# The state-space mixing with channels on partitions, and its roots on VectorE

## The chip, the cores and the metric

The kernel runs on one core of a Trainium2 chip. The metric is the time of one execution on the device in microseconds (us), as the median of several runs. Everything is fp32. The engines are named as the profile names them: PE is TensorE (PEld its weight loads), DVE is VectorE, ACT is ScalarE, POOL is GpSimd and SP is SyncE, which here only starts transfers.

## The reference, cut to what matters

Two layers work on 8 sequences of 256 tokens with 256 features, 2048 tokens in all. After each of the four parts the input is added and a layer norm is taken.

```python
x = layernorm(x + attention(x))              # 16 heads of 128
x = layernorm(x + experts0(x))               # 32 experts, 6 per token, and a shared one
x = layernorm(x + state_space(x))            # the part that the change touches
x = layernorm(x + experts1(x))               # 16 experts, 4 per token, and a shared one

def state_space(x):                          # E = 512 channels, 8 heads of 64, N = 64
    gate, hBC, dt = split(x @ in_proj_w.T)
    h, B, C = split(silu(causal_conv(hBC, 4 taps)))
    dt = softplus(dt + dt_bias);  a = -exp(A_log) * dt
    # per head, over the tokens s <= l of one sequence:
    y[l] = sum_s (C[l].B[s]) * exp(sum of a over s+1..l) * dt[s] * h[s]  +  D * h[l]
    yf = y * silu(gate)
    yn = norm_w * yf * rsqrt(mean(yf * yf over the 512 channels) + 1e-6)
    return yn @ out_proj_w.T
```

The sum over s is taken in blocks of 128 tokens. A sequence has two blocks: within a block a product of matrices, and for the second block the contribution of a state S that the first block leaves (called "the state's part" here).

## The kernel before

The kernel is one program for all of it. Tokens are taken in 4 groups (g) of 512, each of 4 tiles (t) of 128 tokens, so a group holds two sequences. The residual x of a group lies in SBUF with tokens on partitions (`xg[g]`). The order of the work in the program text is written out by hand with generators: `weave` takes several of them, gives each a start and an end on an axis of "slots", and calls them in turn. The tile framework's scheduler then threads the instructions on each engine, so that an engine's order is not quite that of the text; within the finished program every engine's queue runs in order.

**The state-space layer.** `front(g)` prepares a group: transposes x (`turned_group`, L1256), projects and convolves it (`convolved`, L1194 to L1203, channels on partitions), takes the time steps (`time_steps`, L1214 to L1245, a long chain of tiny VectorE steps that ends in `dta`), the decays (`decays`: `edge` L1275, and per tile and four heads a matmul `sg` L1305 with an exponential that gives the block's decay matrix e), the product of B and C (`gm`, L1337) and the gate (`gtp`, L1361, then the silu of L1179). The gate has tokens on partitions, one tile of 128x512 per t. `back(lo, hi)` runs the slots. In slot s, four things are done for four different tiles, s, s-1, s-2 and s-3:

- tile s: transposes h (L1393), multiplies by dt (`hd`, L1399) and, in even tiles, by the decay to the block's end (`hx`, L1405); multiplies e by gm (L1411, twice); in even tiles it forms the state S (L1419, copied by ACT L1424).
- tile s-1: `y`, tokens on partitions: for every pair of heads a matmul of h with `dres`, a diagonal matrix of D (L1438), and on top of it one matmul per head (L1443), with the 128x128 matrix of the head as weights and 64 columns of `hd` streaming. In odd tiles the state's part `yo` (L1451) is scaled by `edge` (L1455) and added (L1460). Then the product with the gate (L1462 or L1464), the square with its sum over the row by ACT (L1469), and its root.
- tile s-2: four transposes of yf (L1484) and ACT's copy `yfT` (L1486).
- tile s-3: the output projection (L1494), the residual with the root as factor (L1498), and the layer norm (`normed`).

A matmul of fp32 is two instructions on PE, a transpose is one. PSUM is given out by tag: "a" 3 banks, "b" 2 (hdp, Sp, yfp, out), "c" 2 (y), "d" 1 (yo).

**Roots.** `normed` (L726) computes 1/sqrt(var + eps). In groups 0 to 2 POOL does it in three steps (L741, L742 with the operation pow, L744), and the root of the squares' mean too (L1475). In the last group `root_by_steps` (L713) does both on VectorE: a first guess by integer arithmetic and three Newton steps, 11 tiny instructions per root. After either, ACT applies it to x (L745).

**Around it.** `all_combined(g)` finishes the first mixture of experts for a group and also calls `normed`. `routed_group(g)` runs `route` for the second mixture, once tile 3 of group g is through: transposes of the new x (L299), logits (L307), the choice, and 16 scatters of rows by POOL (L380), each preceded by POOL's copy of the row (L375). After the slots come the shared expert (`sh1.shared`, and for groups 1 and 2 L552 and L572), the route of group 3, and the routed tiles: SP loads 128 rows per tile, PE works, POOL scatters the result (L680). The weights of the second mixture's experts are loaded into the big buffer `big` by SP as places in it become free: `order` (L1154) names these places, and `load_up_to` after slot s loads as many experts as fit into those that are free by then. A routed tile picks its expert at run time and so needs all of them loaded.

## Time and profile before

| | |
|---|---|
| median of 6 runs | 1513.46 us (1512.56 to 1518.49) |
| the profiled execution | 1512.64 us |
| its span, first to last instruction | 1510.9 us |
| granted TensorE clock, mean | 0.968 |
| PE busy | 1419.3 us (94%) |
| VectorE busy | 816.2 us (54%) |
| ACT busy | 547.4 us (36%) |
| POOL busy | 486.1 us (32%) |

How to read the profile. Times are microseconds from the first instruction of the span. A line of the timeline has start, length, engine, source line, operation, output and inputs, and shape (partitions x elements); in brackets stands how long the engine was idle before it, and what ended the idle time. "x8" means eight instructions merged into one line. A busy PE is modelled, since matmuls overlap; the starts of weight loads are the better clock for it. A group line has busy us, the mean of one in ns, and the idle time before the group's instructions. The granted clock is the share of full speed that TensorE was allowed.

### The profile page before, as it was taken

The numbers are of one execution on the slowest core, as the hardware profiler recorded it, in microseconds if no ns is written. First come the engines' busy times: TensorE is split into PE (matmuls) and PEld (weight loads), VectorE is DVE, ScalarE is ACT, GpSimd is POOL, SyncE is SP. The second block draws the span as 40 slices with busy tenths as digits, with TensorE's granted clock in tenths as the row PEclk, the third lists the DMA queues.
The fourth block names the chain that finished last, engine by engine and source line by source line (L and its number), as shares of the span: only waits on it lengthen the run. The fifth ranks groups of instructions, "written<-read, shape, count | busy, mean of one in ns | idle before, by whom it ended". The sixth has DMA issues, their size and how long they took to land.

```text
span 1510.9 us, 21640 instructions
## 1 busy us (share of the span) xinstructions
PE 1419.3 (94%) x6482; PEld 1010.8 (67%) x6482; DVE 816.2 (54%) x2957; ACT 547.4 (36%) x1447; POOL 486.1 (32%) x736
## 2 busy tenths in 40 slices
PE   8999999999999999997999994899998699999997
PEld 4666666676666666676778883555666577777766
DVE  3444465456544465456455554676674664544436
ACT  3333342333333342334244442455554222333323
POOL 1000003500152001522755664022144555643345
PEclk9999999999999999998999997899998889999999
DMA  9999999930010001343555555310000622333327
GB/s 362 411 413 414 412 407 392 345 77 1 11 53 22 0 1 60 109 152 104 148 183 157 160 167 193 103 65 1 1 25 32 250 102 86 111 108 95 96 75 278
DMA packets 79974, 233.51 MB, mean 155 GB/s; under 512 B 11323, under 2 KB 44378, under 8 KB 78448
## 3 DMA queue, kind: packets, MB, share of 16 engines
q1 hardware_dynamic: 60784, 187.79, 34.8%
q0 software_dynamic: 16768, 42.19, 7.9%
q10 hardware_dynamic: 2304, 2.10, 0.4%
q8 instruction: 56, 0.92, 0.3%
q14 instruction: 62, 0.51, 0.1%
HBM read 80.29 MB, written 155.40 MB: 156 GB/s over the span
## 4 chain that ended last, share of the span: by engine, by line
PE 62%; issue 14%; POOL 13%; DMA 5%; DVE 4%; ACT 1%; POOLq 1%; SPq 0%; ACTq 0%; DVEq 0%
PE qkp L943 15%; PE vp L927 7%; PE op L1009 6%; POOL m1ys L680 5%; PE zp L996 4%; PE sc L963 4%; POOL m1xs L380 3%; PE pt L990 3%; DMA m0ys<-m0ys,m0xl 2%; PE sc L959 2%; PE sg L1305 2%; PE zp L1000 2%; PE cv L1194 2%; POOL m0ys L680 1%; PE gtp L1361 1%
## 5 line engine op out<-in xcount | busy, mean ns | idle before, releaser
L943 PE MATMUL qkp<-xT,big 128*128 128x512 f32 x512 | 241.2, 593 | 0.0
L978 ACT ACTIVATE pr<-neg,least 128x128 f32<-128x128 f32 (+1 forms) x256 | 114.4, 448 | 283.7 <-DVE least L973 283.7
L951 DVE COPY qk<-qkp 128x512 f32<-128x512 f32 x64 | 44.2, 690 | 178.2 <-PE qkp L943 178.1
L943 PEld LDWEIGHTS qkp<-xT,big 128*128 128x128 f32 x512 | 90.7, 191 | 69.4 <-issue 67.9
L680 POOL DMA_INDIRECT m0ys<-m0ys,m0xl x114 | 112.5, 986 | 65.2 <-ACT m0ys L679 26.7
L380 POOL DMA_INDIRECT m0xs<-m0xe,m0rows x96 | 94.8, 987 | 110.1 <-DVE total L982 37.9
L927 PE MATMUL vp<-big,xT 128*128 128x512 f32 x256 | 118.6, 602 | 4.6 <-DVE x L1014 4.6
L1009 PE MATMUL op<-big,z 128*128 128x256 f32 x512 | 120.5, 382 | 0.0
L973 DVE CUSTOM_DVE_ANT_0 neg<-sc,cmask 128x128 f32<-128x128 f32 (+1 forms) x256 | 81.4, 355 | 59.9 <-PE sc L963 59.2
L680 POOL DMA_INDIRECT m1ys<-m1ys,m1xl x74 | 72.8, 984 | 100.0 <-ACT m1ys L679 92.8
L1009 PEld LDWEIGHTS op<-big,z 128*128 128x128 f32 x512 | 92.6, 190 | 14.9 <-ACT z L1031 4.8
L259 POOL TENSOR_TENSOR rstd<-rstd,numbers 128x1 f32<-128x1 f32 x16 | 8.7, 551 | 280.3 <-DVE rstd L258 280.3
L927 PEld LDWEIGHTS vp<-big,xT 128*128 128x128 f32 x256 | 47.3, 193 | 49.8 <-issue 42.5
L996 PE MATMUL zp<-pT,big 128*128 128x256 f32 x256 | 76.8, 381 | 0.1
L963 PE MATMUL sc<-qk,qk 128*128 128x256 f32 x256 | 76.5, 380 | 0.0
L984 DVE TENSOR_SCALAR pr<-pr,total 128x128 f32<-128x128 f32 (+1 forms) x256 | 72.4, 331 | 3.4
L380 POOL DMA_INDIRECT m1xs<-m1xe,m1rows x64 | 63.3, 989 | 19.1 <-POOL m1xe L375 11.9
L990 PEld LDWEIGHTS pt<-ident,pr 128*128 128x128 f32 x384 | 47.4, 142 | 32.4 <-issue 29.8
L994 DVE COPY pT<-pt 128x384 f32<-128x384 f32 x128 | 66.9, 549 | 2.9 <-PE pt L990 2.1
L996 PEld LDWEIGHTS zp<-pT,big 128*128 128x128 f32 x256 | 47.7, 190 | 30.4 <-issue 12.0
L745 ACT ACTIVATE x<-x,off,rstd 128x256 f32<-128x256 f32 x48 | 28.6, 599 | 95.1 <-POOL off L744 82.4
L741 POOL TENSOR_SCALAR rstd<-mv 128x1 f32<-128x1 f32 x44 | 14.4, 329 | 140.6 <-DVE mv L732 99.2
(2809 smaller groups left out, 3093.0 us busy)
## 6 DMA issues: line engine op xcount, KB each, us to landing
m0xs<-blank SPq DMA_DIRECT2D x9, 7740.0 KB, 59.6
m1xs<-blank SPq DMA_DIRECT2D x4, 7740.0 KB, 56.5
m0xl<-m0xs SPq DMA_DIRECT2D x114, 129.0 KB, 2.3
m0gy<-m0ys SPq DMA_DIRECT2D x16, 768.0 KB, 4.3
m1xl<-m1xs SPq DMA_DIRECT2D x74, 129.0 KB, 2.2
big<-m1ys SPq DMA_DIRECT2D x16, 512.0 KB, 6.7
big<-in_w_moe SPq DMA_DIRECT2D x1, 5472.0 KB, 17.4
big<-in_w_heads SPq DMA_DIRECT2D x12, 384.0 KB, 8.0
```

The costliest lines, as they stand in the source:

```text
L380: ins = nc.gpsimd.indirect_dma_start(out=d["xs"], out_offset=bass.IndirectOffsetOnAxis(ap=rows[:, k, t : t + 1], axis=0), in_=xe[:, k, :], ...
L680: ins = nc.gpsimd.indirect_dma_start(out=d["ys"], out_offset=bass.IndirectOffsetOnAxis(ap=row[:, DM : DM + 1].bitcast(I32), axis=0), in_=y ...
L927: nc.tensor.matmul(ps, lhsT=xT[:, k, t * P : (t + 1) * P], rhs=w_vq[q][:, k, :], start=(k == 0), stop=(k == KC - 1),)
L943: nc.tensor.matmul(ps, lhsT=w_qk[h][:, at : at + P], rhs=xT[:, k, :], start=(k == 0), stop=(k == KC - 1),)
L963: nc.tensor.matmul(sc[:, P:], lhsT=qT[:, c0 + P : c0 + SEQ], rhs=kT[:, c0 : c0 + SEQ], start=True, stop=True,)
L973: nc.vector.tensor_tensor_reduce(out=neg[:, cols], in0=sc[:, cols], in1=cmask[:, cols], scale=-SCALE, scalar=3.0e38, op0=ALU.add, op1=ALU.min,
L978: nc.scalar.activation(pr[:, cols], neg[:, cols], AF.Exp, bias=least[:, i : i + 1], scale=-1.0, accum_out=total[:, i : i + 1],)
L984: nc.vector.tensor_scalar_mul(pr[:, cols], pr[:, cols], total[:, i : i + 1])
L990: nc.tensor.transpose(pt[:, i * P : (i + 1) * P], pr[:, i * P : (i + 1) * P], ident)
L994: pace[0] = nc.vector.tensor_copy(pT, pt)
L996: nc.tensor.matmul(zps[:, b * SEQ : (b + 1) * SEQ], lhsT=vs[2 * b][:, cols], rhs=pT[:, : 2 * P], start=True, stop=False,)
L1009: nc.tensor.matmul(ps[:, :DM], lhsT=zs[i][:, t * P : (t + 1) * P], rhs=w_o[q * QH + i], start=(i == 0), stop=(i == QH - 1),)
```

## The change

`y` is now formed with channels on partitions. For each pair of heads j there is a 128x128 region of y: the rows 0 to 63 belong to the even head, 64 to 127 to the odd one. The head's matmul swaps its operands: 64 columns of `hd` are the weights, and the head's 128x128 matrix streams. The diagonal matrix `dres` and its matmuls are gone; VectorE adds D times h to y with one `scalar_tensor_tensor` per pair of heads, four per tile, D being a factor per partition. The state's part is formed a slot earlier, scaled by `edge` into a buffer `o`, and in odd tiles added to y by a matmul with the identity, which transposes it as well. The gate is projected with channels on partitions, for a whole group at once. So yf has channels on partitions, and the output projection takes it as it is: the transposes `yfp` and ACT's copies `yfT` are gone. The sum of squares over the channels is now a sum over partitions: ACT writes the squares, and in slot s PE multiplies those of tile s-2 with a column of ones, four matmuls of one column. All roots of the slots are taken by VectorE: in one slot the root of the squares of tile s-2 and the root of the variance of tile s-3 stand side by side in a 128x2 tile and go through `root_by_steps` together, 14 instructions (11 where only one of them is there). `normed` stays on POOL for the combined tokens. The places in `big` are given out anew: the two buffers `r` move out of it, `o` comes in, the gate takes 8 places instead of 7, and experts are loaded after slots 12 to 17 instead of 12 to 16.

```diff
@@ -712,18 +712,38 @@
     def root_by_steps(y, v):
 
-        work = small.tile([P, 2], F32, name="newton", tag="newton", bufs=1)
-        i, t = work[:, 0:1].bitcast(I32), work[:, 1:2]
+        n = y.shape[1]
+        work = small.tile([P, 4], F32, name="newton", tag="newton", bufs=1)
+        i, t = work[:, :n].bitcast(I32), work[:, 2 : 2 + n]
         nc.vector.tensor_single_scalar(i, v.bitcast(I32), 1, ALU.arith_shift_right)
         nc.vector.tensor_scalar(i, i, -1.0, float(0x5F3759DF), ALU.mult, ALU.add)
-        last = work[:, 0:1]
+        last = work[:, :n]
         for _ in range(3):
-            nc.vector.scalar_tensor_tensor(t, last, v, last, ALU.mult, ALU.mult)
+            if n == 1:
+                nc.vector.scalar_tensor_tensor(t, last, v, last, ALU.mult, ALU.mult)
+            else:
+                nc.vector.tensor_mul(t, last, v)
+                nc.vector.tensor_mul(t, t, last)
             nc.vector.tensor_scalar(t, t, -0.5, 1.5, ALU.mult, ALU.add)
             nc.vector.tensor_mul(y, last, t)
             last = y
 
-    def normed(g, t, by_steps=False):
+    def spread(g, t, var):
+
+        st = small.tile([P, 6], F32, name="st", tag="st")
+        nc.vector.bn_stats(st, xg[g][:, t, :])
+        mv = small.tile([P, 2], F32, name="mv", tag="mv")
+        nc.vector.bn_aggr(mv, st)
+        nc.vector.tensor_scalar_add(var, mv[:, 1:2], LN_EPS)
+        return mv
+
+    def scaled(g, t, mv, rstd):
+        x = xg[g][:, t, :]
+        off = small.tile([P, 1], F32, name="off", tag="lnoff")
+        nc.vector.scalar_tensor_tensor(off, mv[:, 0:1], -1.0, rstd, ALU.mult, ALU.mult)
+        nc.scalar.activation(x, x, AF.Identity, bias=off, scale=rstd)
+
...
@@ -1142,20 +1156,14 @@
         shsb = st.enter_context(tc.tile_pool(name="shsb", bufs=3, reuse_waits="tile"))
         HB = 4
         FRONT, BACK, COMBINE, ROUTE = 24, 36, 8, 20
-
-        dres = act.tile([P, ED // P, P], F32, name="dres", tag="dres")
-        for j in range(ED // P):
-            nc.vector.tensor_scalar_mul(
-                dres[:, j, :], ident, par[:, DRES0 + j : DRES0 + j + 1]
-            )
         ready = set()
 
 
         order, free = [], {}
         for s, names in (
-            (12, "x0 x1 x2 x3 c0 c1 r0 r1 B h0 h1 h2 h3 e8 e9 e10 e11 g2 g3 g4 m0 C0"),
-            (13, "e0 e1 g5"), (14, "e2 e3 g6"), (15, "e4 e5 g0"),
-            (16, "e6 e7 g1 h4 h5 h6 h7 m1 C1"),
+            (12, "x0 x1 x2 x3 c0 c1 B h0 h1 h2 h3 e8 e9 e10 e11 m0 C0"),
+            (13, "e0 e1 g0 g1 g2 g3"), (14, "e2 e3"), (15, "e4 e5"),
+            (16, "e6 e7 h4 h5 h6 h7 m1 C1 o"), (17, "g4 g5 g6 g7"),
         ):
             order += names.split()
             free[s] = len(order)
@@ -1290,7 +1298,7 @@
             f["e"] = {}
             for t in range(GT):
                 for q in range(HS // HB):
-                    r = slots_of("r", 2).rearrange("p (h s) -> p h s", h=HB)
+                    r = act.tile([P, HB, P], F32, name=f"r{g}_{t}_{q}", tag="r", bufs=2)
                     if q:
             yield
-            f["gate"] = []
-            for t in range(GT):
-                ps = bank("a", f"gtp{g}_{t}")
+            assert g < 2 or ("squared", (g - 2) * GT + 3) in ready
+            gate = f["gate"] = slots_of("g", 8, ED // P).rearrange("p (j s) -> p j s", s=GN)
+            for j in range(ED // P):
+                ps = bank("a", f"gtp{g}_{j}")
                 for k in range(KC):
                     nc.tensor.matmul(
-                        ps, lhsT=xT[:, k, t * P : (t + 1) * P], rhs=win[:, k, :ED],
+                        ps, lhsT=win[:, k, j * P : (j + 1) * P], rhs=xT[:, k, :],
                         start=(k == 0), stop=(k == KC - 1),
                     )
-                gt = slots_of("g", 7, last=g * GT + t)
-                curve(gt, ps, AF.Silu, exps, silus)
-                f["gate"].append(gt)
+                curve(gate[:, j, :], ps, AF.Silu, exps, silus)
                 yield
 
...
+                roots = small.tile([P, 2], F32, name=f"roots{s}", tag="roots", bufs=4)
+                has = [1, 1]
                 if s < NG * GT:
                     g, t = divmod(s, GT)
                     assert ("front", g) in ready and (s == 0 or ("slot", s - 1) in ready)
@@ -1424,71 +1435,78 @@
-                if 0 <= s - 1 < NG * GT:
-                    g, t = divmod(s - 1, GT)
-                    f = got[g]
-                    y = bank("c", f"y{g}_{t}")
-                    hd = hds.pop(t)
-                    for q in range(HS // HB):
-                        m = ms.pop((t, q))
-                        for i in range(HB):
-                            h = q * HB + i
-                            j = h // 2
-                            if h % 2 == 0:
-                                nc.tensor.matmul(
-                                    y[:, j * P : (j + 1) * P],
-                                    lhsT=f["h"][j][:, t * P : (t + 1) * P],
-                                    rhs=dres[:, j, :], start=True, stop=False,
-                                )
-                            nc.tensor.matmul(
-                                y[:, h * PD : (h + 1) * PD], lhsT=m[:, i, :], rhs=hd[:, h, :],
-                                start=False, stop=(h % 2 == 1),
-                            )
-                        yield
-                    yf = act.tile([P, ED], F32, name=f"yf{g}_{t}", tag="yf", bufs=2)
-                    if t % 2:
+                    else:
+
                         ps = bank("d", f"yo{g}_{t}")
                         nc.tensor.matmul(
                             ps, lhsT=f["C"][:, t * P : (t + 1) * P], rhs=states.pop(t - 1),
                             start=True, stop=True,
                         )
+                        yo = slots_of("o", 1).rearrange("p (h d) -> p h d", d=PD)
                         nc.vector.tensor_mul(
-                            yf.rearrange("p (h d) -> p h d", d=PD),
-                            ps.rearrange("p (h d) -> p h d", d=PD),
-                            f["edge"][:, t, :].unsqueeze(2).broadcast_to([P, HS, PD]),
+                            yo, ps.rearrange("p (h d) -> p h d", d=PD),
+                            f["edge"][:, t, :].unsqueeze(2).broadcast_to(wide),
                         )
-                        nc.vector.tensor_add(yf, yf, y)
+                        offs[t] = yo.rearrange("p h d -> p (h d)")
                         yield
-                        nc.vector.tensor_mul(yf, yf, f["gate"][t])
-                    else:
-                        nc.vector.tensor_mul(yf, y, f["gate"][t])
+                if 0 <= s - 1 < NG * GT:
+                    g, t = divmod(s - 1, GT)
+                    f = got[g]
+
+                    y = bank("c", f"y{g}_{t}").rearrange("p (j s) -> p j s", s=P)
+                    hd = hds.pop(t)
+                    tok = slice(t * P, (t + 1) * P)
+                    off = offs.pop(t, None)
+                    yf = act.tile([P, ED // P, P], F32, name=f"yf{g}_{t}", tag="yf", bufs=3)
+                    for q in range(HS // HB):
+                        m = ms.pop((t, q))
+                        for j in range(q * HB // 2, (q + 1) * HB // 2):
+                            if off is not None:
+                                nc.tensor.matmul(
+                                    y[:, j, :], lhsT=off[:, j * P : (j + 1) * P], rhs=ident,
+                                    start=True, stop=False,
+                                )
+                            for i in range(2):
+                                h = 2 * j + i
+                                nc.tensor.matmul(
+                                    y[i * PD : (i + 1) * PD, j, :], lhsT=hd[:, h, :],
+                                    rhs=m[:, h - q * HB, :], start=off is None, stop=True,
+                                )
+                        yield
+                    for j in range(ED // P):
+                        nc.vector.scalar_tensor_tensor(
+                            yf[:, j, :], f["h"][j][:, tok], par[:, DRES0 + j : DRES0 + j + 1],
+                            y[:, j, :], ALU.mult, ALU.add,
+                        )
+                        if j == 1:
+                            yield
+                    gate = f["gate"][:, :, tok]
+                    nc.vector.tensor_mul(yf, yf, gate)
                     yfs[t] = yf
+
+                    pace[0] = nc.scalar.activation(gate, yf, AF.Square)
                     ready.add(("mixed", s - 1))
-
-                    rms = small.tile([P, 1], F32, name=f"rms{g}_{t}", tag="rms")
-                    pace[0] = nc.scalar.activation(f["gate"][t], yf, AF.Square, accum_out=rms)
-                    nc.vector.tensor_scalar(rms, rms, 1.0 / ED, RMS_EPS, ALU.mult, ALU.add)
-                    if g == NG - 1:
-                        square, rms = rms, small.tile([P, 1], F32, name=f"rr{t}", tag="rms")
-                        root_by_steps(rms, square)
-                    else:
-                        nc.gpsimd.tensor_tensor(rms, rms, root[:, :1], ALU.pow)
-                    rmss[t] = rms
                     yield
                 if 0 <= s - 2 < NG * GT:
                     g, t = divmod(s - 2, GT)
-                    ps = bank("b", f"yfp{g}_{t}")
-                    yf = yfs.pop(t)
+
+                    ps = bank("b", f"squares{g}_{t}")[:, :1]
+                    square = got[g]["gate"][:, :, t * P : (t + 1) * P]
                     for j in range(ED // P):
-                        cols = slice(j * P, (j + 1) * P)
-                        nc.tensor.transpose(ps[:, cols], yf[:, cols], ident)
-                    yfT = act.tile([P, ED // P, P], F32, name=f"yfT{g}_{t}", tag="yfT", bufs=2)
-                    nc.scalar.copy(yfT.rearrange("p j n -> p (j n)"), ps)
-                    yfTs[t] = yfT
+                        nc.tensor.matmul(
+                            ps, lhsT=square[:, j, :], rhs=ones[:, :1],
+                            start=(j == 0), stop=(j == ED // P - 1),
+                        )
+                    nc.vector.tensor_scalar(
+                        squares[:, 0:1], ps, 1.0 / ED, RMS_EPS, ALU.mult, ALU.add
+                    )
+                    rmss[t] = roots[:, 0:1]
+                    has[0] = 0
+                    ready.add(("squared", s - 2))
                     yield
                 if 0 <= s - 3 < NG * GT:
                     g, t = divmod(s - 3, GT)
-                    yfT = yfTs.pop(t)
+                    yfT = yfs.pop(t)
                     ps = bank("b", f"out{g}_{t}")[:, :DM]
                     for j in range(ED // P):
                         nc.tensor.matmul(
@@ -1498,8 +1516,14 @@
                     nc.vector.scalar_tensor_tensor(
                         xg[g][:, t, :], ps, rmss.pop(t), xg[g][:, t, :], ALU.mult, ALU.add
                     )
-                    normed(g, t, by_steps=g == NG - 1)
+                    mv = spread(g, t, squares[:, 1:2])
+                    has[1] = 2
                     yield
+                if has[0] < has[1]:
+                    cols = slice(*has)
+                    root_by_steps(roots[:, cols], squares[:, cols])
+                if has[1] == 2:
+                    scaled(g, t, mv, roots[:, 1:2])
                 ready.add(("slot", s))
                 load_up_to(M1, free.get(s, 0) * SLOT)
 
```

(In `normed` the branch with `by_steps` is removed; what is left are the POOL steps L741 to L744 and L745.)

More of the change, by code (lines that the diff above doesn't have):

```diff
@@ L724, in root_by_steps, with normed @@
             last = y
-    def normed(g, t, by_steps=False):
+    def spread(g, t, var):
[10 more added lines that the diff above has]
+        nc.scalar.activation(x, x, AF.Identity, bias=off, scale=rstd)
+    def normed(g, t):
         x = xg[g][:, t, :]
@@ L734, in normed @@
         off = small.tile([P, 1], F32, name="off", tag="lnoff")
-        if by_steps:
-            var = small.tile([P, 1], F32, name="var", tag="rstd")
-            nc.vector.tensor_scalar_add(var, mv[:, 1:2], LN_EPS)
-            root_by_steps(rstd, var)
-            nc.vector.scalar_tensor_tensor(off, mv[:, 0:1], -1.0, rstd, ALU.mult, ALU.mult)
-        else:
-            nc.gpsimd.tensor_scalar_add(rstd, mv[:, 1:2], LN_EPS)
-            nc.gpsimd.tensor_tensor(rstd, rstd, root[:, :1], ALU.pow)
-            nc.vector.tensor_scalar_mul(off, mv[:, 0:1], -1.0)
-            nc.gpsimd.tensor_tensor(off, off, rstd, ALU.mult)
+        nc.gpsimd.tensor_scalar_add(rstd, mv[:, 1:2], LN_EPS)
+        nc.gpsimd.tensor_tensor(rstd, rstd, root[:, :1], ALU.pow)
+        nc.vector.tensor_scalar_mul(off, mv[:, 0:1], -1.0)
+        nc.gpsimd.tensor_tensor(off, off, rstd, ALU.mult)
         nc.scalar.activation(x, x, AF.Identity, bias=off, scale=rstd)
@@ L1380, in front @@
             ready.add(("front", g))
-        ms, hds, states, yfs, yfTs, rmss = {}, {}, {}, {}, {}, {}
+        ms, hds, states, offs, yfs, rmss = {}, {}, {}, {}, {}, {}
         def back(lo, hi):
             for s in range(lo, hi):
+                squares = small.tile([P, 2], F32, name=f"squares{s}", tag="squares")
+                roots = small.tile([P, 2], F32, name=f"roots{s}", tag="roots", bufs=4)
+                has = [1, 1]
                 if s < NG * GT:
@@ L1465, in back @@
                     yfs[t] = yf
+                    pace[0] = nc.scalar.activation(gate, yf, AF.Square)
                     ready.add(("mixed", s - 1))
-                    rms = small.tile([P, 1], F32, name=f"rms{g}_{t}", tag="rms")
-                    pace[0] = nc.scalar.activation(f["gate"][t], yf, AF.Square, accum_out=rms)
-                    nc.vector.tensor_scalar(rms, rms, 1.0 / ED, RMS_EPS, ALU.mult, ALU.add)
-                    if g == NG - 1:
-                        square, rms = rms, small.tile([P, 1], F32, name=f"rr{t}", tag="rms")
-                        root_by_steps(rms, square)
-                    else:
-                        nc.gpsimd.tensor_tensor(rms, rms, root[:, :1], ALU.pow)
```

## The prediction

> **What bounds the kernel now.** First the busy time of each engine by stretch of the span. The columns are: stretch and its length in us, then busy us of matmuls, weight loads, VectorE (DVE), ScalarE (ACT) and GpSimd (POOL), each with its number of instructions, the granted TensorE clock, the DMA share and GB/s.
>
> ```profile
> 980.00:1250.00 270.00, 241.69 (x1148) 167.07 (x1147) 178.91 (x653) 122.52 (x258) 98.39 (x190) 0.91 0.19 70
> 1165.00:1197.00 32.00, 31.55 (x193) 24.66 (x192) 25.78 (x126) 14.76 (x35) 12.01 (x23) 1.00 0.57 222
> 1151.00:1163.00 12.00, 12.00 (x42) 8.83 (x43) 4.96 (x16) 3.24 (x10) 1.53 (x4) 0.52 0.00 1
> 1210.00:1224.00 14.00, 13.92 (x47) 10.88 (x46) 6.84 (x60) 4.71 (x9) 6.57 (x12) 0.53 0.22 66
> 1300.00:1460.00 160.00, 160.00 (x775) 118.70 (x774) 72.83 (x214) 50.61 (x128) 66.27 (x68) 1.00 0.33 101
> ```
>
> The state-space slots lie at about 980 to 1250 us. TensorE is busy 241.7 of those 270 us, VectorE 178.9 (66%). From 1300 to 1460, the second mixture of experts, TensorE never stops, so a microsecond that TensorE saves in the slots reaches the end whole, as long as the experts' rows are there in time. Two stretches run at about half clock; the waits and the timeline tell why. A waits line gives us in total, times, the longest.
>
> ```profile
> ACT x L745 <- POOL off L744: 44.6, 13, 12.9
> PE m1xTp L299 <- ACT x L745: 12.7, 2, 12.1
> PE hdp L1393 <- ACT yfT L1486: 4.0, 1, 4.0
> ```
>
> ```profile
> 1203.29 0.98 POOL L380 DMA_INDIRECT m1xs<-m1xe,m1rows  x1 [0.28 <-POOL m1xe L375]
> 1204.64 0.22 POOL L741 TENSOR_SCALAR rstd<-mv 128x1 f32<-128x1 f32 x1
> 1205.03 1.07 POOL L380 DMA_INDIRECT m1xs<-m1xe,m1rows  x1 [0.17 <-DMA m1xs<-m1xe,m1rows]
> 1206.47 0.59 POOL L742 TENSOR_TENSOR rstd<-rstd,numbers 128x1 f32<-128x1 f32 x1
> 1207.37 1.06 POOL L380 DMA_INDIRECT m1xs<-m1xe,m1rows  x1 [0.17 <-issue]
> 1208.81 0.20 POOL L744 TENSOR_TENSOR off<-off,rstd 128x1 f32<-128x1 f32 x1
> ...
> 1209.69 0.69 PE L299 MATMUL m1xTp<-ident,x 128*128 128x128 f32 x2 [12.09 <-ACT x L745]
> ...
> 1149.83 0.60 ACT L745 ACTIVATE x<-x,off,rstd 128x256 f32<-128x256 f32 x1 [8.81 <-POOL off L744]
> 1150.95 0.44 PE L1393 MATMUL hdp<-ident,big 128*128 128x128 f32 x2 [4.04 <-ACT yfT L1486]
> ```
>
> The three tiny steps of a layer norm (L741, L742, L744) stand in POOL's queue among the scatters of the router. The mean and variance were ready at about 1194.3 (bn_aggr starts at 1194.13, 0.18 long), the last POOL step ran at 1208.8. Until then ACT is blocked, and TensorE idle for 12.09 us. At 1147 to 1151 it is the same: ACT stands 8.81 us at the norm, the copy yfT behind it frees no bank, and TensorE waits 4.04 us. After each gap the clock is 0.52 or 0.53 for 12 and 14 us: 0.48 x 12 = 5.8 and 0.47 x 14 = 6.6 us lost. The two stalls cost 12.1 + 6.6 + 4.0 + 5.8 = 28.5 us.
>
> **Part 1: roots leave POOL.** All norms of the slots (groups 0 to 2; group 3 already) get their roots on VectorE. The POOL roots that stay (combined tokens of groups 2 and 3) run before the first scatters at 1117, so none is left behind a scatter. Where does each stall go? At 1194.3 a chain of 14 steps, variance and offset follows. Isolated, VectorE's steps start 0.21 us apart (nine steps from 1197.32 to 1199.21, below): 16 x 0.21 = 3.4, so the norm is ready at 1197.7, ACT's 0.60 ends at 1198.3, and TensorE, dry at 1197.6, waits about 1 us. At 1147 the bank is freed by VectorE instead of ACT, and next late is dta: its chain (L1239, L1240, L1243, L1245) would be done near 1148.1, when TensorE at full clock reaches edge (L1275), plus whatever VectorE newly does before it: I put 3 us. Of 28.5 us, 24.5 are gained.
>
> **Part 2: VectorE's bill.** These lines give the prices: group lines of VectorE (busy us, mean ns) and two steps of a lone root.
>
> ```profile
> L1203 DVE SCALAR_TENSOR_TENSOR big<-cv,par,big 128x510 f32<-128x510 f32 x15 | 11.0, 746 | 5.3 <-ACT big L1200 5.3
> L1498 DVE SCALAR_TENSOR_TENSOR x<-out,rms,x 128x256 f32<-128x256 f32 x12 | 5.8, 480 | 3.6 <-PE out L1494 3.4
> ...
> 1197.32 0.21 DVE L721 SCALAR_TENSOR_TENSOR newton<-newton,rms 128x1 f32<-128x1 f32 x1
> ...
> 1199.21 0.15 DVE L717 TENSOR_SCALAR newton<-var 128x1 int32<-128x1 int32 x1
> ```
>
> Per column (746 - 480) / 254 = 1.05 ns, so one 128x128 step with D is 480 - 128 x 1.05 = 346 ns; followed directly by the next it takes about 0.08 less (hd starts 0.40 after the 0.48 step before it), 0.27. Four take 1.08 to 1.38. An even slot had one 0.69 product and keeps it: +1.08 to 1.38. An odd slot had 0.69 + 0.68 + 0.68 and loses the 0.68 addition: +0.40 to 0.70. Over 8 + 8 slots 11.8 to 16.6, I take 14. Roots: 15 calls of 14 steps and 2 of 11 are 232, against 8 calls of 11 = 88, so +144; alone 0.21 each (30), threaded between other work 0.065 (the start-to-start of small steps at 1186.1; 9); 12 variance additions add 1 to 2. I take 19, in the middle: VectorE's order is already threaded, but not everywhere. Sum +33 (22 to 49): 212 of some 257 us, 82%. What does such a load cost? From 1165 to 1197 VectorE is at 25.8 of 32 us (81%) and TensorE is idle 0.45 us, so the load by itself is hidden. But the dt chain of a group is all VectorE latency: at 1035.79 TensorE waited 1.88 us for dta, and the clock was at 0.5 from 1036 to 1042. Two such points (groups 1 and 2) growing by 2.5 us each: -5 us.
>
> **Part 3: TensorE's bill.** A slot had 8 loads for D, 16 for heads and 4 transposes, 28. It gets 16 for heads and 8 for the sums of squares, and an odd slot 8 more that add the carried state's part: 24 and 32, again 28 on average. Loads set the pace (weight-load timeline):
>
> ```profile
> 1107.64 0.30 PEld L1443 LDWEIGHTS y<-hd,big 128*128 128x128 f32 x2
> ...
> 1110.26 0.30 PEld L1494 LDWEIGHTS out<-wout,yfT 128*128 128x128 f32 x2
> ...
> 1042.44 0.19 PEld L1419 LDWEIGHTS Sp<-hx,Bt 128*64 128x64 f32 x2 [1.41 <-DVE big L1411]
> 1043.44 0.42 PEld L1484 LDWEIGHTS yfp<-ident,yf 128*128 128x128 f32 x4 [0.81 <-issue]
> ```
>
> 24 loads from 1107.64 to 1110.26 are 0.109 each; one-column sums are like dtp (16 in 1.69 us, 0.106). So the count costs nothing. Open is the head's new form: 64 weight columns, 128 moving ones, two heads in two halves of the partitions. Low end: the two 64-column loads of Sp fit into 0.19 us, 0.055 apart; at that pace 16 are 0.88 instead of 1.74: -14 us in all. High end: Sp's 2 x 0.43 took 1.00 until the next load, 0.14 for changing width; an even slot has 4 such changes, an odd one 8, 96 in all: +13. A 128-column stream alone needs 0.107 (a quarter of 0.43), so I stand nearer the high row: +6.
>
> [...]
>
> **Part 4: nothing on the path.** The gate with channels on partitions has the same 64 matmuls and 16 curves. ACT loses 16 copies (0.58) and 16 accumulator reads (0.19), 12 us at 45% load: hidden already, besides the bank above. POOL loses 12 times some 1.9 us, and its scatters still go one in 1.67 us. Group 1's took from 1187 to 1219 and start about 10 us earlier too, so they don't hold up group 2's. SP loads the second mixture's experts as 7, 2, 1, 1, 4, 1 instead of 9, 1, 1, 2, 3; the last goes after slot 17, which ends near 1235. The shared experts' work until 1281 covers it; uncovered it costs its landing time, about 8 us (7.9 for the two-expert load). The state's part (yo) moves one slot ahead: same instructions, waiting for S of the slot before; VectorE's product stands then before y's work, but its 20.6 us of waits on yo lie within the stalls and the drain.
>
> **Sum.** -24.5 + 5 + 6 = -13.5. The profiled execution took 1512.64 us (span 1510.9 + 1.7 around it); that makes 1499.1. The median, 1513.46, is 0.8 above it: 1500.
>
> **Rivals.** *Column halves together* (-14 instead of +6): 1480. For it, a narrow load's 0.055 us; against it, two fp32 passes in each half, and no row with two halves. *VectorE takes POOL's place*: the slots' D steps and roots stand before dt's chain and before the products m and hd that TensorE waits for. At the dear prices VectorE is at 228 of 270 us. Price: each of three groups idles 4 us more and falls to half clock (6.5 x 0.5 = 3.3), and each of 16 slots waits 0.7: 22 + 11; with the width at +13 that is 46 against 28.5 gained: +17, 1531; with the width at +6, 1524. It decides once TensorE loses more than 1.4 us per slot to VectorE. For it, 9.6 of 10 us VectorE at 1000 to 1010; against it, the stretch from 1165. *Roots change queue only*: threaded among other work a root can last long (rms at 1181.58, its root at 1190.32), so the two stalls shrink by half, 14 us, and the 11 us of costs take nearly all: 1510.
>
> **Numbers.** Forecast 0.50, own range 1489 to 1508; halves together 0.14; queue only 0.11, between 1507 and 1514; VectorE 0.25. Changes under 0.2% (3 us) can't be told from none. Faster 0.67 (the first two, and 0.03 of the third); same 0.08; slower 0.25. The range 1482 to 1524 leaves out about 1 in 10 on each side.
>
> **What would show it.** Right: no idle of TensorE over 2 us after 1100, no wait of ACT's L745 step on POOL in the slots, clock 0.95 or more over them, VectorE near 212 us. Wrong: waits of hdp, y or edge on VectorE of 1 us and more in many slots, or head matmuls at 0.06 or 0.15 us instead of 0.11. POOL's scatters of group 2 starting no earlier would show a gain that stays in the slots.

## The result, and the profile after

The changed kernel takes 1522.9 us (median of 20 runs, 1518.01 to 1526.39), the kernel before 1514.39 us in the same comparison (46 runs). The ratio is 1.0052, with a 95% interval of 1.0041 to 1.0062: the change costs 8 us where 13.5 were to be gained. The profiled execution took 1524.6 us; its span is 1522.9 us, 12 us more than before.

First the stretch from the first `hd` to the first routed tile of the second mixture, the part in which the two kernels differ most, in the kernel before and then in the changed one (columns as in the prediction).

```profile
982.00:1282.00 300.00, 272.28 (x1301) 193.44 (x1302) 192.71 (x731) 128.78 (x269) 113.39 (x219) 0.92 0.19 71
```

```profile
984.00:1291.00 307.00, 280.80 (x1304) 185.03 (x1304) 219.86 (x943) 121.89 (x239) 95.96 (x171) 0.91 0.20 69
...
1140.00:1165.00 25.00, 24.68 (x119) 16.14 (x119) 16.35 (x64) 8.36 (x14) 17.81 (x28) 0.86 0.18 64
1165.00:1197.00 32.00, 27.85 (x134) 17.92 (x134) 22.96 (x129) 13.57 (x33) 0.00 (x0) 0.84 0.49 187
1197.00:1225.00 28.00, 22.80 (x109) 16.50 (x109) 21.55 (x88) 5.72 (x9) 21.26 (x34) 0.81 0.45 151
```

The stretch is 7 us longer; of the other 5, 2 lie ahead of it and 2.5 behind it. VectorE has 27 us more, POOL 17 us less. TensorE is idle for 26.2 us (307 - 280.8), hardly less than the 27.7 of before, and the clock is at 0.91 (0.92 before), though both long POOL stalls are gone. What took their place stands in the list of waits (us in total, times, the longest):

```profile
ACT x L744 <- DVE off L743: 21.4, 9, 5.0
...
PE edge L1283 <- DVE roots L728: 5.8, 1, 5.8
PE sg L1313 <- ACT r L1309: 3.1, 3, 1.2
PE edge L1283 <- DVE newton L726: 3.0, 1, 3.0
PE y L1471 <- DVE hd L1410: 2.9, 2, 1.8
PE squares L1496 <- DVE m1s_0h L562: 2.5, 1, 2.5
```

In the slots ACT's step of the norm waits for VectorE now, no longer for POOL. TensorE waits longest at `edge`, for `dta`; that the list names a Newton step there means only that this step ended last before it. The timeline of VectorE, in the kernel before and then in the changed one, shows how `dta` comes to be late:

```profile
1027.40 0.19 DVE L1221 TENSOR_TENSOR dtv<-dtp,par 128x32 f32<-128x32 f32 x1 [1.40 <-PE dtp L1214]
...
1035.54 0.19 DVE L1245 TENSOR_TENSOR dta<-dt,a_neg 128x32 f32<-128x32 f32 x1
```

```profile
1027.48 0.19 DVE L1229 TENSOR_TENSOR dtv<-dtp,par 128x32 f32<-128x32 f32 x1 [2.02 <-PE dtp L1222]
...
1034.30 0.18 DVE L1247 SCALAR_TENSOR_TENSOR dts<-dts,dtz 128x32 f32<-128x32 f32 x1
1034.40 0.16 DVE L719 TENSOR_SCALAR newton<-newton 128x2 int32<-128x2 int32 x1
1034.47 0.34 DVE L1477 SCALAR_TENSOR_TENSOR yf<-big,par,y 128x128 f32<-128x128 f32 x1
1034.73 0.18 DVE L1247 SCALAR_TENSOR_TENSOR dts<-dts,dtz 128x32 f32<-128x32 f32 x1
...
1036.95 0.18 DVE L1247 SCALAR_TENSOR_TENSOR dts<-dts,dtz 128x32 f32<-128x32 f32 x1
1037.05 0.15 DVE L725 TENSOR_TENSOR newton<-roots,squares 128x2 f32<-128x2 f32 x1
1037.12 0.95 DVE L765 TENSOR_TENSOR m0gy<-m0gy 128x768 f32<-128x768 f32 x1
1037.99 0.20 DVE L1248 SCALAR_TENSOR_TENSOR dts<-dts,dtz 128x32 f32<-128x32 f32 x1
...
1039.03 0.18 DVE L1253 TENSOR_TENSOR dta<-dt,a_neg 128x32 f32<-128x32 f32 x1
```

The chain from `dtv` to `dta` begins at the same time in both kernels. Before, it takes 8.1 us; after, 11.6. Between two of its steps (L1247) stand a Newton step and a D step (L1477), and later a Newton step and a step that combines the first mixture's results (L765), so the chain advances once in 0.43 to 1.04 us here, while TensorE is idle. Over the whole chain the D steps and the roots' steps take some 2 us, the combining steps (L765 to L768) 4.1 us; in the kernel before only 0.3 us of combining falls within the chain, the rest runs ahead of it. So the steps that the change adds are not the larger part of what stands in the way. Whether VectorE's longer queue or the new order of its instructions put the combining steps there, no run separates.

The second thing was not on the prediction's list at all. TensorE and its clock around 1088 us (columns: stretch, PE busy, granted clock, DMA share, GB/s), and what it ran there:

```profile
1084.80:1088.20 3.40, 3.40 (x28) 1.00 0.00 0
1088.20:1091.60 3.40, 3.40 (x11) 0.51 0.01 2
1091.60:1095.00 3.40, 3.40 (x29) 0.99 0.00 0
```

```profile
1085.06 1.85 PE L1222 MATMUL dtp<-win,big 128*128 128x8 f32 x16
1086.76 1.03 PE L1496 MATMUL squares<-ones,big 128*128 128x1 f32 x8
1087.66 3.21 PE L1512 MATMUL out<-wout,yf 128*128 128x256 f32 x8
...
1094.64 1.97 PE L1512 MATMUL out<-wout,yf 128*128 128x256 f32 x8
```

TensorE is busy all the time, and yet the clock is halved at 1088.2: the same eight `out` instructions take 3.21 us and then 1.97. Before that it had run 24 matmul instructions of 8 columns and of one (1085.06 to 1087.66). They keep up the pace of their weight loads (0.108 us each), but hardly anything streams. Of the nine places in the stretch where the clock is at half, this is the only one with no idle time of TensorE in the 3.4 us ahead of it; ahead of 1156.5 there were 0.29 us, elsewhere 0.8 us and more.

### The profile page after: what moved, and what is told of

Read it like the earlier page. It is cut to its first block, busy times and chain, and to the rows that moved or that the text cites. A ratio compares the mean times of both kernels' runs of the same rounds, so it can differ in the third digit from the quotient of the medians.

```text
span 1522.9 us, 21753 instructions
## 1 busy us (share of the span) xinstructions
PE 1431.2 (94%) x6482; PEld 1005.4 (66%) x6482; DVE 841.7 (55%) x3165; ACT 540.0 (35%) x1417; POOL 468.2 (31%) x688
## 3 DMA queue, kind: packets, MB, share of 16 engines
q1 hardware_dynamic: 60928, 187.79, 34.8%
## 5 line engine op out<-in xcount | busy, mean ns | idle before, releaser
L380 POOL DMA_INDIRECT m1xs<-m1xe,m1rows x64 | 64.3, 1004 | 20.8 <-POOL m1xe L375 12.5
L973 PEld LDWEIGHTS sc<-qk,qk 128*128 128x128 f32 x256 | 43.7, 190 | 22.4 <-issue 20.2
L1004 PE MATMUL pt<-ident,pr 128*128 128x128 f32 x384 | 58.0, 274 | 0.0
```

What stands on the lines that cost most here:

```text
L380: ins = nc.gpsimd.indirect_dma_start(out=d["xs"], out_offset=bass.IndirectOffsetOnAxis(ap=rows[:, k, t : t + 1], axis=0), in_=xe[:, k, :], ...
L1004: nc.tensor.transpose(pt[:, i * P : (i + 1) * P], pr[:, i * P : (i + 1) * P], ident)
```

## The experiments

Three theories. **A:** VectorE's longer queue makes `dta` late; TensorE idles and then runs at half clock. **B:** TensorE's clock halves where it streams few columns, busy or not, so the one-column sums of squares cost clock. **P:** the prediction's Part 1, POOL's stalls are dear and the roots do well to leave POOL. The runs below were made on five other chips. On each of them the kernel before takes 1543 to 1547 us (the first `hd` comes 24 to 34 us later there than in the profile before; the stretch from `hd` to the routed tiles is the same length in the changed kernel, 307 us); 0.1% is 1.5 us. So I compare ratios to the kernel before. The three kernels that were timed on two chips differ by 0.0006, 0.0015 and 0.0021 in them, so a difference of 3 us between runs of different chips means little.

| kernel | ratio (95%) | stretch, us | PE busy | clock |
|---|---|---|---|---|
| changed kernel, again | 1.0046 (1.0030 to 1.0062) | 307 | 280.6 | 0.91 |
| e1 changed, roots on POOL | 1.0138 (1.0111 to 1.0165) | 318 | 281.5 | 0.90 |
| e2 before, roots on VectorE | 0.9879 (0.9853 to 0.9905) | 281 | 265.3 | 0.96 |
| e3 changed, sums 128 columns | 0.9911 (0.9886 to 0.9936) | 285 | 264.8 | 0.96 |
| e4 changed, no D | 0.9930 (0.9905 to 0.9954) | 290 | 271.9 | 0.95 |
| e5 changed, sums 32 columns | 0.9994 (0.9977 to 1.0010) | 299 | 274.8 | 0.94 |
| e6 e3 and dtp 128 columns | 0.9895 (0.9877 to 0.9913) | 287 | 268.4 | 0.96 |
| e7 e2 and dtp 128 columns | 0.9869 (0.9846 to 0.9892) | 282 | 264.5 | 0.96 |
| e8 e3, no D | 0.9850 (0.9822 to 0.9879) | 276 | 263.9 | 0.98 |
| e9 changed, early dt | 0.9900 (0.9869 to 0.9931) | 285 | 266.7 | 0.96 |
| e10 e7 and early dt | 0.9777 (0.9746 to 0.9809) | 270 | 258.0 | 0.99 |
| e11 e3, heads 128 columns | 0.9836 (0.9805 to 0.9867) | 275 | 261.8 | 0.98 |
| e12 changed, sums 8 columns | 1.0031 (1.0018 to 1.0044) | 304 | 275.3 | 0.93 |
| e13 before, early dt | 1.0061 (1.0039 to 1.0082) | 307 | 268.7 | 0.92 |
| e14 changed, all remedies | 0.9752 (0.9732 to 0.9771) | 266 | 253.9 | 0.99 |

The last three columns come from the windows of each profile, from the first `hd` to the first routed tile. Length less PE busy is TensorE's idle time. The lengths differ by nearly as much as the ratios say (e3: 22 us here, 20.8 by the ratio), so what the edits gain or lose lies in this stretch.

**The base, and the roots alone (e1, e2).**

> The changed kernel itself, as the base for the other edits on this chip. By the ratio of the changed kernel's own comparison, 1.0052, it is expected at 1.004 to 1.0075 of the kernel before. If the chip on which the first four experiments ran is what made them differ, it would show here as another ratio.

As expected, 1.0046.

```diff
 # e1, on the changed kernel (groups 0 to 2)
-                    has[0] = 0
+                    nc.gpsimd.tensor_tensor(roots[:, 0:1], squares[:, 0:1], root[:, :1], ALU.pow)
-                    mv = spread(g, t, squares[:, 1:2]); has[1] = 2
+                    normed(g, t)
 # e2, on the kernel before
-                    normed(g, t, by_steps=g == NG - 1)
+                    normed(g, t, by_steps=True)      # and root_by_steps for every rms
```

> The changed kernel with the slots' roots of groups 0 to 2 put back on POOL (tensor_tensor pow); the new layout, the D step and the gate stay. VectorE loses 12 norm roots and 12 root-mean-square roots. Theory A (VectorE's queue: its added steps stand before dta, hd and the sums, TensorE idles and falls to half clock): the time falls from 1522.9 to 1510-1518, even though ACT again waits 8 us and more on the norm's POOL steps behind the scatters. Theory B (the clock halves because one-column matmuls stream too little): 1521-1525, no change. Theory P (the prediction's Part 1: the POOL stalls are dear, 24 us): 1535 or more.

> The kernel before with one part of the change alone: all roots of the slots by steps on VectorE (one column each, 11 steps for the root-mean-square, 12 with the variance for the norm); token-major output, transposes and D on TensorE stay. Theory P (prediction's Part 1: the two POOL stalls are worth 24.5 us, the added steps little): 1490-1500 against 1514.4. Theory A (VectorE's queue): the gain is eaten by longer waits on VectorE, 1508-1518. Theory B (clock after one-column matmuls): no one-column sums here, so the stalls' gain stays, 1493-1503.

Roots back on POOL cost 0.92%, 14 us; roots on VectorE alone gain the kernel before 1.21%, 18.7 us. P holds both ways, A misses both (for e2, B had forecast the same as P). In e2 the long waits are gone and nothing as long replaces them, though VectorE has 221 us there, as much as in the changed kernel:

```profile
PE m1xTp L299 <- ACT x L745: 2.6, 3, 0.9
...
PE edge L1275 <- DVE dta L1245: 1.4, 1, 1.4
```

So the loss is in the new layout: 1.0046 against 0.9879, 26 us. By the table 11 us of it are idle time of TensorE (26.4 against 15.7) and the rest is clock: 0.91 of 307 us gives up 28 us of full clock, 0.96 of 281 us gives up 11.

**The width of the sums (e3, e5, e12, e15).**

```diff
-    ps = bank("b", f"squares{g}_{t}")[:, :1]
+    ps = bank("b", f"squares{g}_{t}")[:, :P]         # :32 in e5, :8 in e12
-        ps, lhsT=square[:, j, :], rhs=ones[:, :1],
+        ps, lhsT=square[:, j, :], rhs=ones,          # one column of ps is read
```

> The changed kernel with the sums of squares streamed 128 columns wide (the moving operand is the whole 128x128 tile of ones, one column of the result is used). The same loads, the same instructions on all engines; a 128-column stream keeps to the pace of its load (0.109 us). Theory B: the windows in which TensorE was busy but streamed few columns no longer count as idle, the half-clock spells at 1088, 1156 and 1238 us go, some 7 to 15 us of half clock less, so the time falls by 3 to 8 us to 1515-1520. Theory A: 1521-1525.

> The changed kernel with the sums of squares streamed 32 columns wide instead of 1 or 128: a dose between the changed kernel and the one with 128 columns. Theory B (TensorE counts as idle for the clock while it is busy with loads and streams few columns): time and half clock in between, but nearer to the changed kernel, some 2 to 8 us faster than it, since 32 columns stream for a quarter of each load's pace. Theory A (VectorE's queue): like the changed kernel within 2 us. If the 128-column version was faster only because its order of instructions came out differently, this one may fall anywhere.

> The changed kernel with the sums of squares 8 columns wide. The order in which instructions stand on the engines is planned from their sizes, so every edit so far also moved other instructions; this one moves a like number of them (513 lines of VectorE's order differ, 658 in the 128-column version) while TensorE streams hardly more. If the wide sums won by the chance of the new order, this one may fall anywhere from 0.985 to 1.01. Theory B: 1.002 to 1.006, like the changed kernel.

1, 8, 32 and 128 columns give 1.0046, 1.0031, 0.9994 and 0.9911: the more TensorE streams, with the same number of loads, the shorter the time. B has the direction and the order; for 128 columns it was sized far too small (3 to 8 us expected, 20.8 measured). Every edit also moves the planned order. By the traces e5 puts 364 of TensorE's 6482 matmul instructions in another place, e3 413, and e12 only 102; e5 gains 8 us and e3 20.8, so a new order as such isn't the cause, though it may have a part in e3's gain: 6 of the 22 us by which its stretch is shorter are idle time, among them the 3.0 us at the last `edge`. In e3 the place of the halved clock shown above reads as follows (the sums begin at 1117.14):

```profile
1116.10:1119.40 3.30, 3.30 (x25) 1.00 0.01 2
1119.50:1122.90 3.40, 3.40 (x29) 1.00 0.00 0
```

The probe puts the question to TensorE alone:

```diff
+    for n in (128, 64, 128, 32, 128, 16, 128, 1, 128):
+        ps = bank("a", "probe")
+        for _ in range(100):
+            nc.tensor.matmul(ps[:, :n], lhsT=xg[NG - 1][:, GT - 1, :P], rhs=ones[:, :n],
+                             start=True, stop=True)
```

> The changed kernel and behind its end nine stretches of 100 matmuls each on TensorE with nothing else running: moving operands of 128, 64, 128, 32, 128, 16, 128, 1 and 128 columns, same weights, results not used. Theory B: TensorE is busy all the time, yet the granted clock falls to half in the stretches of 1 and 16 columns, stays at full in those of 128, and 64 and 32 tell where it turns; at full clock a stretch takes some 22 us. If the clock halves only when TensorE has nothing to do, all nine stay at full clock after the first 10 us.

The windows lie within the nine stretches, in their order (128, 64, 128, 32, ... columns):

```profile
1546.00:1569.60 23.60, 23.60 (x199) 0.93 0.05 18
1570.00:1591.60 21.60, 21.60 (x196) 1.00 0.00 1
1592.00:1614.00 22.00, 22.00 (x199) 1.00 0.01 1
1618.20:1653.00 34.80, 34.80 (x165) 0.50 0.00 0
1659.20:1678.00 18.80, 18.80 (x170) 1.00 0.00 1
1683.10:1716.60 33.50, 33.50 (x159) 0.50 0.00 1
1720.60:1741.00 20.40, 20.40 (x185) 1.00 0.00 1
1744.50:1780.00 35.50, 35.50 (x168) 0.50 0.00 1
1785.50:1805.00 19.50, 19.50 (x176) 1.00 0.00 1
```

TensorE is busy throughout. With 128 and 64 columns the clock is at 1.00 (0.93 in the first window) and an instruction goes in 0.11 us (22.0 / 199); with 32, 16 and one it is at 0.50, and an instruction takes 0.21 (34.8 / 165). B is shown: the clock halves although TensorE is busy, and in this probe it turns between 32 columns (0.50) and 64 (1.00).

**VectorE's load (e4, e8).** The D step is left out: `yf = y * gate`, one product as before.

> The changed kernel without the D term (it leaves out D times h; the gate multiplies the mixing's output straight from PSUM): VectorE loses 64 steps of 0.34 us, 19 to 22 us, and nothing else changes. Theory A: 1508-1517, and TensorE's waits on VectorE in the slots shrink. Theory B: 1520-1523. If the added D steps cost nothing (the prediction's 'hidden by itself'): 1521-1525.

> The changed kernel with sums of squares 128 columns wide and without the D term (it leaves out D times h). With narrow sums, leaving out D brought the ratio to the kernel before from 1.0046 to 0.993 (18 us). If D's 20 us on VectorE act by themselves (theory A, added to B), the gain repeats: 0.9911 - 0.0116 = 0.979 to 0.981. If they mattered because each small wait on VectorE pushed a window with narrow sums under what the clock wants, most of that gain is gone once the sums are wide: 0.986 to 0.991.

Without D the changed kernel gains 18 us (1.0046 to 0.9930), and the clock goes from 0.91 to 0.95 although the sums are as narrow as ever. With wide sums the same edit gains 9 us (0.9911 to 0.9850). TensorE's idle time falls by 8 us both times (26.4 to 18.1, and 20.2 to 12.1); what differs is the clock. So D's steps are not hidden (A), and about half of their price hung on the narrow sums. For the same 8 us of idle time the clock rises by 0.04 with one-column sums and by 0.02 (0.96 to 0.98) with wide ones; why it does so is not shown.

**The dt chain (e9, e13, e10).**

```diff
-            if g == 0:
-                yield from steps_of(g)
+            yield from steps_of(g)
             yield from inner(g)
-            if g > 0:
-                yield from steps_of(g)
```

> The changed kernel with each group's dt steps made before the convolutions (as for group 0) instead of after them; sums stay one column wide, and ACT changes its table twice more in a group. Theory A in the form of the rival of the prediction (the dt chain, late on VectorE, is what TensorE waits for): TensorE's waits of 5.8 and 3.0 us at the edges of groups 1 and 3 go with the half clock after them, 8 to 15 us, ratio to the kernel before 0.995 to 1.000. Theory B (narrow sums): half clock at the slots' sums stays, 1.001 to 1.005.

> The kernel before with one edit: each group's dt steps ahead of the convolutions. In the changed kernel this edit brought the ratio from 1.0046 to 0.990. If a late dta was as dear before the change, this kernel gains as much, 0.983 to 0.988, and the changed kernel's loss is not dta's. If the change made dta dear, as its VectorE steps stand before the dt steps (theory A), this kernel gains little: TensorE waited 1.88 us at one edge, and the two POOL stalls stay; 0.994 to 1.000.

> The kernel before with roots on VectorE, a 128-column dt projection and dt steps ahead of the convolutions: a candidate for the fastest version. Its TensorE is idle for 7 to 8 us in the slots without the early steps, and at half clock for some 10 to 17, so at most 8 us are left to gain; more table changes on ACT may cost some of it. Expected ratio to the kernel before 0.982 to 0.988, against 0.9869 without the early steps.

e9 gains 1.46%, 22 us, half as much again as A had expected; TensorE's waits at `edge` are gone, its idle time is 8 us less (26.4 to 18.3), and the clock is at 0.96 with one-column sums. In the kernel before the same edit costs 0.6%: a miss for both forecasts. Its waits show POOL's stalls grown, 12.9 and 12.3 us where 12.1 and 4.0 were (ACT, which TensorE waits for, stands 16.7 and 13.3 us at the norm's POOL step):

```profile
ACT x L745 <- POOL off L744: 51.9, 14, 16.7
...
PE gtp L1361 <- ACT big L1179: 12.9, 1, 12.9
PE hdp L1390 <- ACT yfT L1483: 12.3, 1, 12.3
PE m1xTp L299 <- ACT x L745: 7.3, 4, 5.1
```

So e13 can't tell what `dta` cost before. e10 against e7, where the roots have left POOL, tells what it costs in the old layout with the roots on VectorE: 0.9869 to 0.9777, 14 us, more than the 8 that were expected at most. A late `dta` is thus dear in both layouts. That it is dearer in the new one, 22 us against 14, isn't shown: each of the two differences is good to some 6 us.

**The dt projection and the head's form (e6, e7, e11).**

```diff
 # e6 (on e3) and e7 (on e2): 128 columns, the last 8 of each 128 are used
-    ps[:, t * HS : (t + 1) * HS], ... rhs=win[:, k, PROJ - HS :]
+    ps[:, t * P : (t + 1) * P], ... rhs=win[:, k, PROJ - P :]
 # e11 (on e3)
-    y[i * PD : (i + 1) * PD, j, :], lhsT=hd[:, h, :], ...
+    y[:, j, :], lhsT=<hd of heads 2j and 2j+1, 128 columns>, ... start=... and i == 0, stop=i == 1
```

> The changed kernel with the sums of squares 128 columns wide and the dt projection (32 matmuls of 8 columns, in the changed kernel as in the one before) 128 columns wide too; only the 8 dt columns of each are used. Theory B: the half clock that stays at each group's dt projection (10 us at about 1068 in the 128-column version) goes as well, so 2 to 8 us less than with wide sums alone: ratio to the kernel before 0.985 to 0.990. Theory A: as with wide sums alone, 0.991, since dta is as late as ever.

> The kernel before with the roots on VectorE (ratio 0.988) and its dt projection 128 columns wide. Theory B: half clock at the dt projection goes, ratio 0.983 to 0.987. Theory A: unchanged, 0.988. It is also a candidate for a version faster than both kernels.

> The changed kernel with wide sums, and each head's matmul given 128 weight columns (both heads of a pair) instead of 64, so that no two run side by side and no tile width changes; the pair's products are summed, so y holds another sum than the mixing's. The prediction's Part 3 took the 64-column form for 6 us dearer than 128 columns: then this is 4 to 8 us faster than wide sums alone, 0.986 to 0.989. If the halves run together (0.055 us each, with some 0.2 us at each change of width), it is 3 to 10 us slower, 0.993 to 0.998.

e6 and e7 are 0.0016 and 0.0010 below their bases, inside the intervals: nothing is settled on the dt projection alone. e11 misses both forecasts: it is some 12 us faster than e3. Yet in an even slot the narrow form is much the shorter, as the timelines of e3 and e11 show:

```profile
1145.63 1.09 PE L1471 MATMUL y<-big,hd 128*64 128x128 f32 x16
1146.65 1.16 PE L1496 MATMUL squares<-ones,big 128*128 128x128 f32 x8
```

```profile
1139.95 1.95 PE L1471 MATMUL y<-big,hd 128*128 128x128 f32 x16
1141.74 1.06 PE L1497 MATMUL squares<-ones,big 128*128 128x128 f32 x8
```

Sixteen take 1.02 us until the next matmul in the narrow form (0.064 each), 1.79 in the wide one (0.112). A stream of 128 columns alone was estimated at 0.107 in the prediction, so at 0.064 the two halves overlap. In an odd slot, where two matmul instructions with the identity and four of the heads take turns, it is the other way round, 0.78 us for such a six in e3 and 0.67 in e11:

```profile
1209.78 0.49 PE L1465 MATMUL y<-ident,big 128*128 128x128 f32 x2
...
1210.56 0.49 PE L1465 MATMUL y<-ident,big 128*128 128x128 f32 x2
```

```profile
1195.88 0.38 PE L1465 MATMUL y<-ident,big 128*128 128x128 f32 x2
...
1196.55 0.39 PE L1465 MATMUL y<-ident,big 128*128 128x128 f32 x2
```

In sum the wide form gives TensorE more to do, and yet e11 is faster: its idle time falls from 20.2 to 13.2 us and its clock rises from 0.96 to 0.98. That the planned order moved too, and what part it has, this run can't tell.

**All remedies (e14), and the two layouts side by side.** e14 has wide sums, wide dt projection, early dt steps, and in odd slots the four matmuls with the identity in a row ahead of the heads.

> The changed kernel with all remedies: sums of squares and dt projection 128 columns wide, dt steps ahead of the convolutions, and in odd slots the four matmuls that add the carried state's part in one row ahead of the heads (fewer changes of tile width). If the remedies for the clock (B) and for dta (A) add up: 0.9895 - 0.0146 = 0.975 or less; if both remove the same half clock: 0.980 to 0.988. The fastest version so far is the kernel before with roots on VectorE, wide dt projection and early dt steps, 0.9777.

Early dt steps and wide columns add up: 0.9752, 45 us less than the changed kernel by the ratios (2.9% of 1544), TensorE idle for 12 us of 266 at a clock of 0.99.

> The changed kernel with all remedies once more (0.9752), beside the kernel before with the same remedies (next run). If the new layout is worth something by itself, as the 8 to 14 us of weight loads that its head pairs may save, it stays 3 us or more ahead; if its D steps on VectorE take that back, both lie within 3 us.

> The kernel before with roots on VectorE, wide dt projection and early dt steps once more (0.9777): the old layout with the same remedies. If the layout itself is neutral, 0.974 to 0.978; if the new layout is the better one, 0.978 to 0.981.

f1 (e14 again) gave 0.9767 (0.9740 to 0.9794), f2 (e10 again) 0.9798 (0.9768 to 0.9829); medians 1507.53 and 1513.53 us. The new layout is ahead both times, by 0.3%, as was forecast if it is the better one, but the intervals overlap. Both versions are 2% faster than either kernel of this case, f2 only by the middle of its interval.

## Why the prediction was wrong

- **Part 1 was right.** ACT's wait on POOL is gone, and the roots' move, steps on VectorE included, is worth 18.7 us in the old layout and 14 in the new one. The prediction's 24.5, less the 5 us that it put on VectorE's bill, lies near that.
- **Part 2 had the bill and not the price.** VectorE's 27 us more fit the forecast of 33 (22 to 49). One step that failed is "the load by itself is hidden": D's steps alone are worth 18 us. It was read from a stretch (1165 to 1197) in which VectorE was 81% busy and TensorE wasn't held up, but that stretch lies behind the last `dta` (1152.8), so no dt chain runs in it. The waits at `edge` themselves came out near what was put: 5.8, 0.6 and 3.0 us in place of 1.9, 0.3 and none, 7.3 us more, where the sum has 2.5 each for groups 1 and 2 and 3 for the last (in Part 1). What has no price in the sum is the half clock that comes with the two long waits, 10.3 us at 0.50 each (1037.0 to 1047.3, 1166.7 to 1177.0); with it, moving the dt steps forward is worth 22 us, 8 of them idle time.
- **Part 3 failed at "the count costs nothing".** The pace of the loads was right (24 instructions of 8 and 1 columns in 1084.8 to 1088.2, at full clock), but a price per instruction leaves out that the transposes that went away streamed 128 columns and the sums that came stream one. Wide sums give back 20.8 us, the largest term that the sum had at nothing. The columns of a slot are the same in total, 8 x 128 + 16 x 64 + 4 x 128 = 2560 for D, heads and transposes before, and 16 x 128 + 8 x 1 with 8 x 128 in odd slots, 2568 on average, after: it isn't the total that fell, but the narrow ones now stand in a row. The head's form, put at +6, came out slightly below nothing: an even slot saves 0.77 us (1.79 - 1.02), an odd one loses four times 0.11 (0.78 - 0.67), some 2.5 us saved over eight of each.
- **Part 4** wasn't contradicted: from the first routed tile to the end it takes 229.1 us before and 231.6 after. (Over all the runs this last part takes 229 to 236 us, in either layout.) That the scatters of group 1 would start 10 us earlier, and group 2's with them, was wrong: they start at 1199.8 and 1243.2 instead of 1187.0 and 1231.4.
- **The rivals.** *VectorE takes POOL's place* (1524 to 1531) came nearest, for a reason half its own. It alone put a price on the half clock behind a wait; but the long waits are at `dta`, not 0.7 us in every slot, and much of the half clock came from the sums (0.91 over the stretch, 0.96 once they are wide). *Column halves together* is what the trace shows (0.064 us a head matmul in e3), but with what the odd slots lose (four times 0.11 us in each) it is worth those 2.5 us, not 14.
- **The signs** did their work: the clock of 0.91 instead of 0.95, and the idle 3.03 us at 1168 and 2.53 at 1221, say by themselves that the sum had failed. (The sign "no idle over 2 us after 1100" sat ill with Part 1, which itself put 3 us on the last `dta`.)

The gains are more than the loss: 20.8 (sums), 22 (dt) and 18 us (D) against the 26 that the layout lost. D's gain and the sums' overlap, since D's falls to 9 us once the sums are wide. The dt steps' gain doesn't overlap with the sums' (45 us in e14, which has two smaller edits besides, where the two together have 43), and part of it is time that the old layout with its roots on VectorE loses too (14 us in e10).

## What to carry to other kernels

Price a TensorE instruction twice, by its pace and by what it streams: where one-column work of the same pace took the place of 128-column work here, the clock was at 0.51 for 3.4 us behind it and the dt projection's 8 columns, and widening it again cost little as long as the loads set the pace (eight sums take 0.91 us at one column and 0.99 at 128). VectorE, at 72 to 79% of the stretch (changed kernel and e2), did not hide what was added to it (D's steps cost 18 us), since a chain of dependent steps on it feeds TensorE, which bounds; look for such a chain (here `dta`) and move it earlier before adding to its queue. Judge an edit by idle time and clock of the stretch together: of the 26 us that the new layout lost, some 11 are idle time and the rest is clock.

## What was not expected of the hardware

- TensorE's clock halved while it was busy without a gap: in the probe it is at 0.50 with 32, 16 and one columns and at 1.00 with 64 and 128 (0.93 in the first window), and in the changed kernel at 0.51 from 1088.2 to 1091.6, with no idle time in the 3.4 us ahead. Short waits came with half clock too: 1.88 us before the change (0.50 from 1036 to 1042) and 3.03 after (0.50 from 1166.7 to 1177.0).
- Two fp32 head matmuls of 64 weight columns, which write the two halves of y's partitions, overlap: 16 instructions in 1.02 us until the next of another width (0.064 each), against 1.79 (0.112 each) for 128 weight columns.
